# A graph-network step on one core: raw groups normalised by VectorE, and one group more brought by VectorE

## The chip, the core and the metric

The kernel runs on one core of a Trainium2 chip. The core has five engines that run their own instruction queues in order: TensorE (PE; its weight loads are PEld), VectorE (DVE), ScalarE (ACT), GpSimd (POOL) and SyncE (SP). The metric is the time of one execution in device microseconds (us). Before the change it was measured three times; the median counts. One further execution was profiled.

## The reference

12500 nodes have 128 features each; 400000 edges, sorted by their destination, have 32 features each. Each node is normalised and cut at zero, a message is made for every edge from its source, its destination and its own features, the messages of a destination are summed, and a GRU makes the new node.

```python
h = jnp.maximum(_layernorm(x, axis=-1), 0.0)
def _L0_gnn_ref(x, ei, ea, w1, b1, w2, b2, w_ih, b_ih, w_hh, b_hh):   # called with x = h
    s, d = (ei[0], ei[1])
    h = jnp.concatenate([x[s], x[d], ea], axis=-1)
    m = jax.nn.relu(h @ w1 + b1) @ w2 + b2
    agg = jax.ops.segment_sum(m, d, num_segments=x.shape[0])
    gi = agg @ w_ih + b_ih
    gh = x @ w_hh + b_hh
    i_r, i_z, i_n = jnp.split(gi, 3, axis=-1)
    h_r, h_z, h_n = jnp.split(gh, 3, axis=-1)
    r = jax.nn.sigmoid(i_r + h_r)
    z = jax.nn.sigmoid(i_z + h_z)
    n = jnp.tanh(i_n + r * h_n)
    return (1.0 - z) * n + z * x
out = x + _L0_gnn_ref(h, edge_index, edge_attr_32, ...)
```

## The kernel before

**Tiles, groups, units.** The edges are cut into 3125 tiles of 128 (T). Eight tiles are a group (PAIR); the first group has five. There are 391 groups (NP), and each is worked in two units, so a group k has the units u = 2k and 2k + 1, 782 in all (NU). The main loop runs over u. A stage of the work on a group is put a fixed number of units ahead of u: the order of every engine's queue is written out by hand (manual_schedule), and each engine works through it in order.

**A first pass over the nodes** (to about 90 us) loads x, normalises it, keeps the normalised features turned in SBUF (hT_all, 128 features x 12500 nodes), and stores A = h times the first 128 rows of w1 in DRAM.

**How a group gets the part of its messages that depends on the source.** There are four ways.
- Most groups are gathered: GpSimd issues one indirect DMA per tile (L170), which brings 128 rows of A, 512 bytes each, into a buffer G. There are eleven such buffers (GBUFS), and a gather waits until the group that had its buffer eleven places before in the ring has been used. VectorE then adds the rows to the product in PSUM and cuts at zero (L748, which writes RB).
- The first nine groups (RAW) are gathered from x itself, since A is not there yet. These are the raw groups. They need the layer norm again: raw_stats takes mean and variance of each tile on VectorE (L227, L229) and the root on ScalarE (L234), raw_fin makes scale and shift by six small VectorE instructions (L240 to L247), raw_h applies them with the cut at zero on ScalarE (relu_norm, L292, 128 columns at a time), raw_turn turns the tiles on TensorE into a PSUM bank (misc, L699) and copies that to SBUF on VectorE (gt, L701), and pre multiplies them by w1a (L727). Their cut at zero into RB is done by ScalarE (L760).
- 30 groups are brought by ScalarE, which copies single columns of hT_all, 1024 to a group (L1062, one_by_one), and 31 by VectorE, which takes two columns with one instruction (L1021, Pairs.pairs, 512 to a group) and sorts their bytes with a copy for each 128 columns (L1032). The index of each column is loaded into registers first, 32 to a load for VectorE. TensorE multiplies them by w1a, and VectorE cuts at zero (L743).
- Five groups are brought by SyncE, one DMA per row.

SPREAD says how many groups each of the three engines brings, START from which unit on it brings the first. Which groups these are follows from both: they lie evenly over the run. A group brought by VectorE must be ready at unit 2k - 6, and pairs_due spreads its 512 pairs evenly over the units since the one before. The others are GpSimd's: 325 before.

**Stages.** stages(u) puts into the queues, in this order: raw_stats(u + 7), raw_fin(u + 6) and raw_h(u + 6), raw_turn(u + 4), the products pre(u + 3), pairs before a long pass (before_long), the one-hot tiles of two groups ahead (L615, L666), the add or cut for u + 2, and pairs and a load behind it (behind_long). The main loop calls ScalarE's copies (run_jobs) in four parts around it, then the segment sums on TensorE (seg, L774), and take (L783), and every 14 groups a node step (node, 28 and a last one): sigmoid and tanh on ScalarE (L861, L873, L875), products on TensorE, and some eight passes on VectorE (L865 to L892). The loop starts at unit -7, so that the raw groups' first stages are worked ahead.

Of the kernel before, what the change touches and what calls it, by code (L numbers as in the profile page):

```python
# [9 lines left out]
F32 = mybir.dt.float32  # L10
# [7 lines left out]
ALU = mybir.AluOpType  # L18
# [5 lines left out]
GRP = 4  # L24
PAIR = 2 * GRP
# [19 lines left out]
RAW = 9  # L45
# [8 lines left out]
STEP = {"act": 4, "sp": 4}  # L54
QUEUE = 10
ROW = 4 * D
SPREAD = {"dve": 31, "act": 30, "sp": 5}
START = {"dve": 8, "act": -6, "sp": 8}
NR = 12672

H_AT = 16512
# [3 lines left out]
def tile_gnn(ctx: ExitStack, tc: tile.TileContext, x, src, srcT, dstT, dstP, eaT, eaP, w1, b1, w2T, b2,  # L65
             wih, bih, whh, bhh, out):
    nc = tc.nc
# [5 lines left out]
    p2 = ctx.enter_context(tc.tile_pool(name="p2", bufs=2))  # L73
# [4 lines left out]
    ps1 = ctx.enter_context(tc.tile_pool(name="ps1", bufs=1, space=bass.MemoryType.PSUM))  # L78
# [7 lines left out]
    def unit_tiles(u):  # L86
        k, h = divmod(u, 2)
        t0, t1 = tiles(k)
        return [(t0 + a * GRP + j, j, a) for j in (2 * h, 2 * h + 1) for a in range(2)
                if t0 + a * GRP + j < t1]  # L90

    mode, order = {}, {m: [] for m in SPREAD}
    for m, n in SPREAD.items():
        lo, hi = START[m] // 2 + 2, NP - {"dve": 5, "act": 3, "sp": 12}[m]
        for i in range(n):
# [32 lines left out]
    ident = const.tile([128, 128], F32, name="ident")  # L128
# [94 lines left out]
    def bn(pool, xs, P, n):  # L223
        b = pool.tile([128, 8, 6], F32, name="bn")
        mv = pool.tile([128, 8, 2], F32, name="mv")
        for j in range(n):
            nc.vector.bn_stats(b[:P, j, :], xs(j))  # L227
        for j in range(n):
            nc.vector.bn_aggr(mv[:P, j, :], b[:P, j, :])  # L229
        return mv  # L230

    def bn_sqrt(pool, mv, P, n):
        s = pool.tile([128, 8], F32, name="s")
        nc.scalar.activation(s[:P, :n], mv[:P, :n, 1], AF.Sqrt, bias=eps[:P, :])  # L234
        return mv, s

    def bn_fin(pool, st, mvs, P, n):
        mv, s = mvs
        y = pool.tile([128, 8], F32, name="y")
        nc.vector.reciprocal(y[:P, :n], s[:P, :n])  # L240
        v = pool.tile([128, 8], F32, name="v")
        nc.vector.tensor_scalar(v[:P, :n], mv[:P, :n, 1], 1e-5, -0.5, op0=ALU.add, op1=ALU.mult)
        nc.vector.tensor_tensor(v[:P, :n], v[:P, :n], y[:P, :n], op=ALU.mult)
        nc.vector.tensor_tensor(v[:P, :n], v[:P, :n], y[:P, :n], op=ALU.mult)
        nc.vector.scalar_tensor_tensor(st[:P, :n, 0], v[:P, :n], 1.5, y[:P, :n],
                                       op0=ALU.add, op1=ALU.mult)
        nc.vector.scalar_tensor_tensor(st[:P, :n, 1], mv[:P, :n, 0], -1.0, st[:P, :n, 0],  # L247
                                       op0=ALU.mult, op1=ALU.mult)
# [42 lines left out]
    def relu_norm(o, xi, st):  # L291
        nc.scalar.activation(o, xi, AF.Relu, bias=st[:, 1:2], scale=st[:, 0:1])  # L292
# [90 lines left out]
    with tc.tile_pool(name="pp", bufs=3) as pp:  # L383
# [22 lines left out]
        mvs, asb = {}, {}  # L406
# [186 lines left out]
    Ls, OH, RT, HE, SEG = ({} for _ in range(5))  # L593
# [14 lines left out]
    def onehot_T(k):  # L608
        if k >= NP:
            return  # L610
        c = slice((k % QP) * 512, (k % QP + 1) * 512)
        o, i = Ls[k // QP][:2 * V, c], Ls[k // QP].bitcast(I32)[:2 * V, c]
        n = k - BLOCKS[-1][0]
        if n < 0:
            nc.vector.tensor_scalar(o, i, node_of[:, k:k + 1], None, op0=ALU.is_equal)  # L615
        else:
            nc.vector.tensor_scalar(o, i, node_of[:, k:k + 1], 0.0, op0=ALU.is_equal, op1=ALU.add,
                                    accum_out=dlast[:2 * V, n:n + 1])
# [50 lines left out]
    def unit(u):  # L669
        k, h = divmod(u, 2)  # L670
        return G[k][:, 2 * h:2 * h + 2, :, :].rearrange("p j a f -> p (j a) f")


    def slots(u):
        return [(j % 2) * 2 + a for _, j, a in unit_tiles(u)]

    def raw_h(u):
        if u < 2 * RAW:
            for i, s in enumerate(slots(u)):
                relu_norm(unit(u)[:, s, :], unit(u)[:, s, :], HE[u][:, i, :])  # L680

    def raw_stats(u):
        if u < 2 * RAW:
            l = slots(u)
            HE[u] = bn_sqrt(p2, bn(p2, lambda j: unit(u)[:, l[j], :], 128, len(l)), 128, len(l))

    def raw_fin(u):
        if u < 2 * RAW:
            n = len(slots(u))
            st = p2.tile([128, GRP, 2], F32, name="st_raw", bufs=4)  # L690
            bn_fin(p2, st[:, :n, :], HE[u], 128, n)
            HE[u] = st

    def raw_turn(u):
        if u < 2 * RAW:
            l = slots(u)
            pt = ps1.tile([128, 512], F32, name="misc")
            for i, s in enumerate(l):
                nc.tensor.transpose(pt[:, i * 128:(i + 1) * 128], unit(u)[:, s, :], ident)  # L699
            hT = p3.tile([128, 512], F32, name="gt", bufs=3)  # L700
            nc.vector.tensor_copy(hT[:, :len(l) * 128], pt[:, :len(l) * 128])  # L701
            HE[u] = hT

    PP = {}
# [1 line left out]
    def pre(u):  # L706
        if u >= NU:
            return
        k, h = divmod(u, 2)
        if h == 0:  # L710
            PP[k] = ps2.tile([128, PAIR, D], F32, name="pre")
        p = PP[k][:, GRP * h:GRP * h + GRP, :]
        for i in range(2):
            c0 = (k % QP) * 512 + (2 * h + i) * 128
            raw = u in HE or k in hand
            nc.tensor.matmul(p[:, 2 * i:2 * i + 2, :], Ls[k // QP][:, c0:c0 + 128], RW[k % 4],  # L716
                             start=True, stop=not raw)
            if raw:
                l = unit_tiles(u)
                for n, (t, j, a) in enumerate(l):  # L720
                    if j % 2 == i:
                        if k in hand:
                            c = (a * GRP + j) * 128
                            cols = hand[k][:, c:c + 128]
                        else:
                            cols = HE[u][:, n * 128:(n + 1) * 128]
                        nc.tensor.matmul(p[:, 2 * i + a, :], cols, w1a, start=False,  # L727
                                         stop=n + 1 == len(l) or l[n + 1][1] != j)
# [28 lines left out]
    def relu(u):  # L757
        if u in RT:
            o, p = RT.pop(u)
            nc.scalar.activation(o, p, AF.Relu)  # L760
# [308 lines left out]
    def pairs_due():  # L1069
        start, n = START["dve"], 0  # L1070
        for k in order["dve"]:
            end = 2 * k - 6
            for u in range(start, end):
                due[u] = n + -(-(PAIR * 64 * (u + 1 - start)) // (end - start))
            n += PAIR * 64
            start = end
# [3 lines left out]
    def behind(u):  # L1080
        return due.get(u, cols.end if u >= START["dve"] else 0) - cols.done

# [4 lines left out]
    def before_long(u, ops):  # L1087
        if u == START["dve"]:
            cols.load()
        some(u, cols.end, QUEUE - ops)  # L1090
        if cols.turn and u % 2 == 0:
            some(u, cols.end, QUEUE - ops - 1)
            cols.part()

    def behind_long(u, least):
        if behind(u) >= least:
            cols.pairs(cols.left())
            cols.load()
# [9 lines left out]
    for m in ("act", "sp"):  # L1108
        start = START[m]
        for k in order[m]:  # L1110
# [39 lines left out]

    def stages(u):
        if u + 7 >= 0:
            raw_stats(u + 7)
        if u + 6 >= 0:
            raw_fin(u + 6)
            raw_h(u + 6)
        if u + 4 >= 0:
            raw_turn(u + 4)
        if u + 3 >= 0:
            pre(u + 3)  # L1160
        before_long(u, 2 if u % 4 == 2 else 1)
        if u % 2 == 0:
            onehot_T(u // 2 + 3)
            onehot(u // 2 + 3)
        if u + 2 >= 0:
            add(u + 2)
            relu(u + 2)
        behind_long(u, 1)

    nc.vector.tensor_scalar(at[:ROWS, :], at[:ROWS, :], place_of[:, 0:1], place_of[:, 1:2],  # L1170
                            op0=ALU.mult, op1=ALU.add)
    for u in range(-7, 0):
        run_jobs(u, 0)
        stages(u)
        for phase in range(1, PH):
            run_jobs(u, phase)
# [16 lines left out]
    for u in range(NU):  # L1193
        k, h = divmod(u, 2)
        gathers(u)
        if h == 0:
# [14 lines left out]
            if k == NP - 20:  # L1211
                check_windows()
        run_jobs(u, 0)
        stages(u)
        run_jobs(u, 1)
        some(u, 4, QUEUE - 1)
# [188 lines left out]
```

## Time and profile before

| | us |
|---|---|
| three runs | 3355.47, 3372.85, 3372.74 |
| their median | 3372.74 |
| the profiled execution, its own time | 3356.5 |
| its span, first to last instruction | 3354.7 |
| busy: TensorE, VectorE, ScalarE, GpSimd | 2383.9, 2429.4, 3232.5, 2509.1 |
| granted TensorE clock, share of full | 0.812 |

A row of a group reads: line, engine, operation, tile written <- tiles read, count | busy time in us, mean ns of one | idle time of the engine right before such instructions, and what ended it. A row of a wait reads: engine, tile and line that waited <- engine, tile and line that ended the wait: us in total, how often, the longest. A row of the timeline reads: start, length in us, instruction, and in brackets the idle time ahead of it. "issue" means that the engine waited for nothing that the profile shows; loads into registers are not counted as busy and appear there. A row of windows gives busy time and count of the engines in a stretch, then the granted clock, the busy share of the DMA engines and GB/s.

### The profile page before, as it was taken

How to read it: one execution, taken by the hardware profiler on the slowest of the kernel's cores; microseconds unless marked ns; L12 is line 12 of the kernel's file. 1: busy time of each engine (PE TensorE's matmuls, PEld its weight loads, DVE VectorE, ACT ScalarE, POOL GpSimd, SP SyncE). 2: the span in 40 equal slices, each digit the busy share in tenths (PEclk: the TensorE clock that was granted, in tenths of full speed). 3: DMA queues.
4: the chain of work that ended last, by engine and by line, in shares of the span. 5: the costliest groups of instructions: out<-in, count | busy, mean ns of one | idle time of the engine just before them, and what ended most of it. 6: DMA issues, size and time to landing. Idle time of an engine off the chain costs nothing. (4 is left out here: it accounts for less than half of the span.)

```text
span 3354.7 us, 98027 instructions
## 1 busy us (share of the span) xinstructions
PE 2383.9 (71%) x13209; PEld 1538.6 (46%) x13209; DVE 2429.4 (72%) x18411; ACT 3232.5 (96%) x31050; POOL 2509.1 (75%) x2606
## 2 busy tenths in 40 slices
PE   7567777766776777677677676776776676767767
PEld 6444444444444454444444444444444444434444
DVE  8467777777767777777777777767777777777775
ACT  6899999999999999999999999999999999999996
POOL 7657777777777777777777777777777777777776
PEclk9777887878877888778888878877887888888888
DMA  6323444444444443434444344444444434444332
GB/s 212 100 69 84 104 98 102 93 103 99 99 94 100 96 99 94 105 90 98 101 97 100 94 101 99 96 93 101 97 98 100 102 96 95 99 99 100 92 97 72
DMA packets 195246, 332.94 MB, mean 99 GB/s; under 512 B 68682, under 2 KB 117385, under 8 KB 194587
## 3 DMA queue, kind: packets, MB, share of 16 engines
q0 software_dynamic: 83104, 170.36, 23.3%
q1 hardware_dynamic: 111339, 156.21, 17.1%
q14 instruction: 549, 4.50, 0.4%
q8 instruction: 110, 1.80, 0.2%
q10 hardware_dynamic: 144, 0.07, 0.0%
HBM read 306.13 MB, written 20.24 MB: 97 GB/s over the span
## 5 line engine op out<-in xcount | busy, mean ns | idle before, releaser
L1062 ACT COPY HE_act<-hT_all 128x4 uint8 x30720 | 3094.2, 189 | 56.7 <-issue 29.6
L170 POOL DMA_INDIRECT G<-A,src_i x2528 | 2442.0, 966 | 806.0 <-issue 747.7
L1021 DVE SCALAR_TENSOR_TENSOR both<-hT_all 128x4 uint16 x15872 | 1353.8, 153 | 693.6 <-issue 653.6
L716 PE MATMUL pre<-RW,L 128*128 128x256 f32 x3128 | 1101.7, 476 | 9.5 <-DMA RW<-B 9.5
L774 PE MATMUL seg<-RB,OH 128*32 128x129 f32 x6250 | 599.7, 322 | 627.5 <-DVE RB L748 477.6
L716 PEld LDWEIGHTS pre<-RW,L 128*128 128x128 f32 x3128 | 646.3, 231 | 284.3 <-issue 213.1
L774 PEld LDWEIGHTS seg<-RB,OH 128*32 128x32 f32 x6250 | 330.9, 124 | 920.0 <-DVE RB L748 550.9
L748 DVE CUSTOM_DVE_ANT_0 RB<-pre,G 128x1024 f32<-128x1024 f32 (+1 forms) x317 | 383.2, 1209 | 32.0 <-PE pre L716 19.0
L615 DVE TENSOR_SCALAR L<-L,node_of 64x512 f32<-64x512 int32 x382 | 186.7, 489 | 12.0 <-DMA L<-in_dstP 12.0
L666 DVE TENSOR_TENSOR OH<-dloc,seg 128x512 f32<-128x512 f16 (+1 forms) x198 | 131.1, 662 | 0.0
L851 PE MATMUL nd<-DEG,brow 34*128 34x512 f32 (+2 forms) x112 | 72.0, 726 | 82.8 <-ACT gt L861 81.2
L806 PE MATMUL misc<-spot_h,dcol 128*128 128x40 f16 x382 | 47.4, 192 | 88.3 <-DVE dcol L831 86.3
L801 PE MATMUL nd<-spot,sums 128*128 128x40 f32 x782 | 98.7, 290 | 14.2 <-DVE sums L783 12.3
L1032 DVE COPY HE_dve<-both 128x512 uint8<-128x512 uint8 x248 | 107.5, 434 | 0.0
L801 PEld LDWEIGHTS nd<-spot,sums 128*128 128x128 f32 x782 | 93.9, 198 | 22.0 <-DVE sums L783 13.0
L727 PEld LDWEIGHTS pre<-w1a,HE_dve 128*128 128x128 f32 x496 | 87.1, 220 | 9.8
L727 PEld LDWEIGHTS pre<-w1a,HE_act 128*128 128x128 f32 x480 | 84.4, 219 | 14.2 <-ACT HE_act L1062 4.7
L727 PE MATMUL pre<-w1a,HE_act 128*128 128x128 f32 x480 | 84.3, 303 | 4.1 <-ACT HE_act L1062 4.1
L727 PE MATMUL pre<-w1a,HE_dve 128*128 128x128 f32 x496 | 86.1, 302 | 0.0
L806 PEld LDWEIGHTS <-dcol 128*128 128x128 f16 x382 | 38.8, 105 | 101.9 <-DVE dcol L831 93.8
L170 POOL DMA_INDIRECT G<-in_x,src_i x69 | 65.6, 951 | 22.2 <-issue 20.7
L743 DVE TENSOR_SCALAR RB<-pre 128x1024 f32<-128x1024 f32 x61 | 74.0, 1213 | 4.7 <-PE pre L727 4.6
(180 smaller groups left out, 1389.0 us busy)
## 6 DMA issues: line engine op xcount, KB each, us to landing
G_sp<-A SPq DMA_DIRECT2D x5120, 0.5 KB
L<-in_dstP SPq DMA_DIRECT2D x195, 256.0 KB
L<-in_eaP SPq DMA_DIRECT2D x195, 256.0 KB
G<-A,src_i POOLq DMA_INDIRECT x2528, 2.5
RW<-B SPq DMA_DIRECT2D x782, 16.0 KB
xb<-in_x SPq DMA_DIRECT2D x26, 256.0 KB
out<-xb SPq DMA_DIRECT2D x26, 256.0 KB
xs<-in_x SPq DMA_DIRECT2D x11, 512.0 KB
```

The costliest lines, as they stand in the source:

```text
L170: fetched = nc.gpsimd.indirect_dma_start(out=G[k][:, j, a, :], out_offset=None, in_=table, in_offset=bass.IndirectOffsetOnAxis(ap=src_i[c] ...
L615: nc.vector.tensor_scalar(o, i, node_of[:, k:k + 1], None, op0=ALU.is_equal)
L666: nc.vector.tensor_tensor(p, dloc[:, e0:e1, None].to_broadcast(shape), row[:, None, :].to_broadcast(shape), op=ALU.is_equal)
L716: nc.tensor.matmul(p[:, 2 * i:2 * i + 2, :], Ls[k // QP][:, c0:c0 + 128], RW[k % 4], start=True, stop=not raw)
L727: nc.tensor.matmul(p[:, 2 * i + a, :], cols, w1a, start=False, stop=n + 1 == len(l) or l[n + 1][1] != j)
L748: made = nc.vector._custom_dve(TENSOR_ADD_SAT, out=o, in0=p, in1=G[k].rearrange("p j a f -> p (j a) f")[:, c, :], s0=float("inf"), s1=0.0)
L774: nc.tensor.matmul(p[r0:r0 + V, :D + 1], OH[k][:, a * GRP + j, :], RB[k % 2][:, 2 * j + a, :D + 1], start=False, stop=all(b != a for _, _, ...
L801: nc.tensor.matmul(p[:, bass.ds(offs[i], V + SHIFT)], sums[:, slot(b, i), :D], spot[:, i % 2, :], start=False, stop=i == len(offs) - 1)
L806: nc.tensor.matmul(p[:, bass.ds(offs[i], V + SHIFT)], t[:, c:c + 128], spot_h[:, a, :], start=False, stop=i == len(offs) - 1)
L1021: nc.vector.scalar_tensor_tensor(self.both[:, e % PIECE // 2, :], column(second), 256.0, column(first), op0=ALU.mult, op1=ALU.add)
L1032: nc.vector.tensor_copy(hand[k].bitcast(U8)[:, p0 * 4:(p0 + PIECE) * 4].rearrange("p (n c b) -> p n c b", c=2, b=4), both.bitcast(U8).rear ...
L1062: nc.scalar.copy(he[:, e * 4:e * 4 + 4], column(v))
```

## The change

VectorE, not ScalarE, applies scale and shift to the raw groups, with one tensor_scalar for each tile; the cut at zero moves to the copy behind the transposes, which becomes a tensor_scalar with a maximum. Statistics, roots and scales are made for two units at a time, at even units. The statistics are put eight units ahead instead of seven, the roots stand in stages of their own a unit behind, and the first statistics are put ahead of the loop. The copy of turned tiles goes from raw_turn to raw_copy at the end of a stage, ahead of behind_long. VectorE brings 32 groups and GpSimd gathers 324; VectorE's first pairs are made from unit 10 on, not 8. Its groups are now 18, 30, 42, 54, ... 374, 386; the first is 18 and the last 386 in both kernels. Where a number is already taken, some of ScalarE's 30 groups shift by one; SyncE's stay.

```diff
-SPREAD = {"dve": 31, "act": 30, "sp": 5}
-START = {"dve": 8, "act": -6, "sp": 8}
+SPREAD = {"dve": 32, "act": 30, "sp": 5}
+START = {"dve": 10, "act": -6, "sp": 8}
...
+    def raw_stats(u):
+        if u % 2 == 0 and u < 2 * RAW:
+            l = [(v, s) for v in (u, u + 1) for s in slots(v)]
+            HE[u] = bn(p2, lambda i: unit(l[i][0])[:, l[i][1], :], 128, len(l)), len(l)
+
+    def raw_sqrt(u):
+        if u % 2 == 0 and u < 2 * RAW:
+            mv, n = HE[u]
+            HE[u] = bn_sqrt(p2, mv, 128, n), n
+
+    def raw_fin(u):
+        if u % 2 == 0 and u < 2 * RAW:
+            mvs, n = HE[u]
+            st = p2.tile([128, PAIR, 2], F32, name="st_raw")
+            bn_fin(p2, st[:, :n, :], mvs, 128, n)
+            HE[u], HE[u + 1] = st[:, :len(slots(u)), :], st[:, len(slots(u)):, :]
+
     def raw_h(u):
         if u < 2 * RAW:
             for i, s in enumerate(slots(u)):
-                relu_norm(unit(u)[:, s, :], unit(u)[:, s, :], HE[u][:, i, :])
-
-    def raw_stats(u):
-        if u < 2 * RAW:
-            l = slots(u)
-            HE[u] = bn_sqrt(p2, bn(p2, lambda j: unit(u)[:, l[j], :], 128, len(l)), 128, len(l))
-
-    def raw_fin(u):
-        if u < 2 * RAW:
-            n = len(slots(u))
-            st = p2.tile([128, GRP, 2], F32, name="st_raw", bufs=4)
-            bn_fin(p2, st[:, :n, :], HE[u], 128, n)
-            HE[u] = st
+                nc.vector.tensor_scalar(unit(u)[:, s, :], unit(u)[:, s, :], HE[u][:, i, 0:1], HE[u][:, i, 1:2],
+                                        op0=ALU.mult, op1=ALU.add)
 
     def raw_turn(u):
         if u < 2 * RAW:
             l = slots(u)
-            pt = ps1.tile([128, 512], F32, name="misc")
+            HE[u] = ps1.tile([128, 512], F32, name="misc")
             for i, s in enumerate(l):
-                nc.tensor.transpose(pt[:, i * 128:(i + 1) * 128], unit(u)[:, s, :], ident)
+                nc.tensor.transpose(HE[u][:, i * 128:(i + 1) * 128], unit(u)[:, s, :], ident)
+
+    def raw_copy(u):
+        if u < 2 * RAW:
+            n = len(slots(u)) * 128
             hT = p3.tile([128, 512], F32, name="gt", bufs=3)
-            nc.vector.tensor_copy(hT[:, :len(l) * 128], pt[:, :len(l) * 128])
+            nc.vector.tensor_scalar(hT[:, :n], HE[u][:, :n], 0.0, None, op0=ALU.max)
             HE[u] = hT
...
     def stages(u):
         if u + 7 >= 0:
-            raw_stats(u + 7)
+            raw_sqrt(u + 7)
+        raw_stats(u + 8)
         if u + 6 >= 0:
             raw_fin(u + 6)
             raw_h(u + 6)
...
             relu(u + 2)
+        if u + 4 >= 0:
+            raw_copy(u + 4)
         behind_long(u, 1)
...
+    raw_stats(0)
     for u in range(-7, 0):
         run_jobs(u, 0)
         stages(u)
```

## The prediction

> **What bounds the kernel now.** I read the busy shares first, then the idle time of each engine and what ended it, and then single stretches of the timeline.
>
> ```profile
> span 3354.7 us, 98027 instructions
> PE 2383.9 (71%) x13209; PEld 1538.6 (46%) x13209; DVE 2429.4 (72%) x18411; ACT 3232.5 (96%) x31050; POOL 2509.1 (75%) x2606
> ...
> L1062 ACT COPY HE_act<-hT_all 128x4 uint8 x30720 | 3094.2, 189 | 56.7 <-issue 29.6
> L170 POOL DMA_INDIRECT G<-A,src_i x2528 | 2442.0, 966 | 806.0 <-issue 747.7
> L1021 DVE SCALAR_TENSOR_TENSOR both<-hT_all 128x4 uint16 x15872 | 1353.8, 153 | 693.6 <-issue 653.6
> ```
>
> ScalarE is full: its copies leave 56.7 us of idle time in the whole run. GpSimd shows 75%, but its gathers are issued back to back. VectorE shows 72%, but 653.6 us of its idle time stands in front of the pair instructions of L1021 and is ended by "issue": it waits there for no other engine, but for its own loads of 32 registers. So three engines are near their limits, and the question is which of them has slack, and where.
>
> ```profile
> core 0: us, PE busy (x) PEld busy (x) DVE busy (x) ACT busy (x) POOL busy (x), PEclk, DMA share, GB/s
> 130.00:200.00 70.00, 47.55 (x272) 37.79 (x268) 38.33 (x237) 69.77 (x534) 43.14 (x46) 0.78 0.30 72
> 290.00:3300.00 3010.00, 2153.18 (x11936) 1359.80 (x11937) 2212.25 (x17103) 2952.11 (x29011) 2288.12 (x2368) 0.81 0.41 98
> ```
>
> In the raw stage (130 to 200 us) ScalarE alone is busy, 69.77 of 70 us; VectorE has 38.33, TensorE 47.55. From 290 us on ScalarE is busy 2952.11 of 3010 us.
>
> ```profile
> POOL G L170 <- issue: 768.5, 2519, 0.6
> POOL G L170 <- DVE RB L748: 21.5, 18, 12.1
> POOL G L170 <- PE misc L699: 16.1, 5, 4.0
> ...
> POOL G L170 <- ACT G L292: 1.7, 1, 1.7
> ...
> 231.38 0.95 POOL L170 DMA_INDIRECT G<-A,src_i  x1 [12.06 <-DVE RB L748]
> ...
> 3337.08 0.94 POOL L170 DMA_INDIRECT G<-A,src_i  x1 [0.30 <-issue]
> ...
> 3345.04 0.44 ACT L950 ACTIVATE gt<-pre 128x320 f32<-128x320 f32 x1 [19.85 <-PE pre L931]
> ```
>
> GpSimd waits for buffers of G for 21.5 + 16.1 + 1.7 = 39.3 us in 24 gaps; 0.3 us of each is its usual gap, so 32 us are true stalls, nearly all before 270 us. Its last gather is issued at 3337.08, 17 us before the end, so GpSimd also ends late. ScalarE's last copies are over some 20 us before 3345.
>
> ```profile
> DVE gt L865 <- ACT gt L861: 40.7, 11, 6.2
> DVE RB L748 <- PE pre L716: 19.0, 10, 4.3
> DVE RB L748 <- DMA G<-A,src_i: 12.7, 4, 4.4
> L743 DVE TENSOR_SCALAR RB<-pre 128x1024 f32<-128x1024 f32 x61 | 74.0, 1213 | 4.7 <-PE pre L727 4.6
> ```
>
> This is all that VectorE waits for others in the long stage that could vanish: 40.7 + 19.0 + 12.7 + 4.6 = 77 us. The first two come from a late ScalarE (a sigmoid queued behind its copies, and TensorE held up by it), the third from GpSimd. VectorE's slack is thus 77 us in 3100, 2.5%.
>
> **Part 1, normalising moves to VectorE, roots are halved.**
>
> ```profile
> L1062 ACT COPY HE_act<-hT_all 128x4 uint8 x340 | 34.0, 190 | 0.2
> L292 ACT ACTIVATE G<-G,st_raw 128x128 f32<-128x128 f32 x32 | 13.1, 478 | 0.0
> L760 ACT ACTIVATE RB<-pre 128x1024 f32<-128x1024 f32 x5 | 5.0, 1000 | 0.0
> L234 ACT ACTIVATE s<-mv,eps 128x4 f32<-128x4 f32 x8 | 2.3, 293 | 0.0
> L240 DVE RECIPROCAL y<-s 128x4 f32<-128x4 f32 x6 | 1.1, 178 | 19.3 <-ACT s L234 19.3
> ...
> ACT s L234 <- DVE mv L229: 4.6, 1, 4.6
> ```
>
> The first four rows are ScalarE from 142 to 193 us, eight units: 51 us, 6.4 each. The rows sum to 54.4, as records overlap a little; 51 / 54.4 = 0.94 puts them on the clock. L292 goes (13.1 x 0.94 / 8 = 1.5 a unit), half of the roots go (0.14), so a raw unit costs ScalarE 4.7. Up to unit 10 that is 61 tiles at 0.385 (23.5 us), some five roots (1.4) and the 4.6 us in which it waited for the first statistics, which are now made a unit earlier: 29 us. With all 69 tiles and nine roots it is 34. TensorE is no obstacle: 47.55 / 70 x 6.4 = 4.3 a unit. VectorE spends 38.33 / 70 x 6.4 = 3.5 a unit there and waits 19.3 us in six units for roots. Gone is half of the six small instructions (0.5 a unit); new are four normalisations of 128 columns. No row has them; between the 0.147 us of an aggregation and the 0.489 of the 64x512 pass I take 0.2, close to the statistics of the same tile:
>
> ```profile
> L227 DVE BATCH_NORM_STATS2 bn<-G 128x6 f32<-128x128 f32 x69 | 14.9, 273 | 0.0
> L229 DVE BATCH_NORM_AGGREGATE mv<-bn 128x2 f32<-128x6 f32 x167 | 14.1, 147 | 0.0
> L615 DVE TENSOR_SCALAR L<-L,node_of 64x512 f32<-64x512 int32 x382 | 186.7, 489 | 12.0 <-DMA L<-in_dstP 12.0
> ```
>
> That makes 3.5 - 0.5 + 0.8 = 3.8 a unit, under ScalarE's 4.7: hidden. At 0.489 it is 5.0, and VectorE would set the unit at a loss of 0.3 x 16 = 5 us; without any cover the 69 instructions cost 14 us (10 to 34). So part 1 gives -29, between -34 and -22 (29 less 5, and 2 for the price of a normalisation). The roots asked a unit ahead wait for nothing new. Behind a root in ScalarE's queue stand the copies of its unit, but the statistics are one unit old by then.
>
> **Part 2, turned tiles copied at a stage's end.** The copy from PSUM (18 of them) gets a maximum instead of a plain copy; the same kind of pass at twice the size takes 1.213 us, so about 0.65, as now. It stands behind the one-hot tiles and the pairs, so VectorE no longer stops for the transposes; the next unit's transposes need its PSUM bank, and wait for it at most that unit's rest. 0, between -5 (one such wait of 4.7 in the raw stage) and +3.
>
> **Part 3, pairs start at unit 10, not 8.**
>
> ```profile
> 182.03 0.60 DVE L1021 SCALAR_TENSOR_TENSOR both<-hT_all 128x4 uint16 x7 [1.79 <-issue]
> ```
>
> VectorE made its first pairs at 182 us, in unit 8. Now its first group has 20 units instead of 22. Up to unit 30 that is 46 pairs more than it had there, 3 loads' worth, against statistics that are over: +4 us by the prices of part 4. In this stretch VectorE is the full engine, so these stand on the path.
>
> **Part 4, one group from GpSimd to VectorE.** GpSimd loses 8 gathers of 0.966 + 0.304 us, 10.2 us. VectorE gains 512 pairs. By the rows: 1353.8 / 31 = 43.7 us of instructions, 653.6 / 31 = 21.1 us of stall, and the eight copies of L1032, 107.5 / 31 = 3.5; 68 us. The add is replaced by a pass of the same length (1.213 against 1.209), nothing. What one more load costs is bounded by these:
>
> ```profile
> L748 DVE CUSTOM_DVE_ANT_0 RB<-pre,G 128x1024 f32<-128x1024 f32 (+1 forms) x317 | 383.2, 1209 | 32.0 <-PE pre L716 19.0
> L1032 DVE COPY HE_dve<-both 128x512 uint8<-128x512 uint8 x248 | 107.5, 434 | 0.0
> ...
> 1506.64 0.60 DVE L1021 SCALAR_TENSOR_TENSOR both<-hT_all 128x4 uint16 x7 [1.33 <-issue]
> ...
> 1513.44 0.60 DVE L1021 SCALAR_TENSOR_TENSOR both<-hT_all 128x4 uint16 x7 [0.27 <-issue]
> ```
>
> A load behind a one-hot pass leaves 0.27 us open, one behind nothing but pairs and a short copy 1.33. The places behind long passes are shared by more loads now, so 32 loads cost between the average (21) and 32 x 1.33 = 43: the group costs 68 to 90, plus an eighth (9 to 11) for the 64 pairs made ahead of unit 10 until now. I take 78, of which 4 are part 3, since the same code that places 31 groups' loads behind long passes places these; 74 remain beyond unit 30, at most 97.
>
> What hides them are the 77 us of waits above: VectorE comes later, so ScalarE's sigmoids and GpSimd's rows are there. Net 0 if all goes, +20 if one load in two is fully exposed and none of the rest is hidden better. But ScalarE has no slack either (2952.11 of 3010 us). Two full engines that meet at 28 node steps don't lag in the same stretches: the waits now come up to 6.2 us each; I estimate one or two such swings that are not absorbed, +8, between 0 and +30.
>
> **A rule that speaks against it.** Gathers take longer while VectorE makes pairs:
>
> ```profile
> L170 POOL DMA_INDIRECT G<-A,src_i x39 | 36.8, 945 | 23.6 <-PE misc L699 12.9 <-issue 10.7
> ...
> L170 POOL DMA_INDIRECT G<-A,src_i x158 | 152.5, 965 | 48.2 <-issue 46.7 <-DVE RB L748 0.3 <-DVE both L1021 0.3
> ```
>
> They take 945 ns from 140 to 200 us and 965 from 700 to 900. The Trainium skill, "SBUF — State Buffer", section "Who interferes with whom", says that VectorE in a two-port mode (a copy or a tensor_scalar) locks GpSimd out of the port they share for the whole instruction, descriptors of its DMAs included. By that rule the 69 normalisations could delay GpSimd by 69 x 0.2 = 14 us; the 20 ns agree with the direction, not with whole instructions. GpSimd's own limit would then be -28 instead of the -42 of the next part, still below the sum, so it would touch only the rival that runs to all limits.
>
> **The sum.** The profiled execution took 3356.5 us, span 3354.7. Limits alone: GpSimd -10 - 32 = -42, ScalarE -34, VectorE -29 + 78 - 77 = -28. With the steps in order: -29 + 0 + 4 + 74 - 74 (of the 77) + 8 = **-17**, or 3339.5 us. The three runs are 3355.47, 3372.85 and 3372.74; the profiled one is like the lowest, 16 below the median, and the page doesn't show what sets the others apart. I give 3345, between 3339.5 and its counterpart 17 higher, nearer the first.
>
> **Rivals.**
> A, every engine runs to its limit: the waits of VectorE vanish and nothing swings. ScalarE's -34 decides, 3322 us (3328 by the rule of the skill). For it: GpSimd never waits after 270 us. Against: two saturated queues that meet.
> B, the start gain is eaten: VectorE's extra 74 to 97 us find only 60 of cover, since VectorE and ScalarE wait for each other in turn. -25 + 14 to 37 + 8 = -3 to +20: 3357 to 3389 with the two kinds of run, no change that can be told. For it: the waits sit at few places (11 and 10). That TensorE, 4.3 us of work in a raw unit, stretches these to 5.5 gives the same: half of the 29 gone.
> C, slower: VectorE becomes the bound for the whole run. The mechanism: each of the 36 added loads (32 and the four of part 3) lies bare at 1.33 us, 101 us in all, the 40.7 us of waits on sigmoids stay, as ScalarE's steps are still queued behind its copies, and only 36 go. -22 + 101 - 36 = +43: 3399 us. It decides when VectorE's extra exceeds its vanished waits by more than 29 + 17 = 46. For it: VectorE's true slack is only 2.5%, and a group is 2.2 to 2.9%. Against: a ScalarE that is 25 us ahead isn't late at the sigmoids.
>
> **Chances.** Forecast (3325 to 3356) 0.40; A 0.08; B 0.33; C 0.19. A measurement of this kernel tells 0.5% (17 us) from no change, so faster means below 3356 and slower above 3389. The upper end of the forecast reads as no change in a run of the slower kind (0.02): faster 0.46, same 0.35, slower 0.19. The range reaches from A's limit, 3320, to C's 3399.
>
> **What would show it.** Right: raw units of about 4.7 us on ScalarE; the first add of L748 near 205 instead of 230 us; GpSimd's stalls on L699 and L748 near nothing; L865's wait on L861 well under 40.7 us; stall ahead of L1021 some 25 to 45 us more. Wrong: a raw unit above 5.5 us, waits of ScalarE that weren't there (for TensorE or HE_act), a wait on L861 as before, or gathers above 980 ns.

## The result, and the profile after

| | kernel before | changed kernel |
|---|---|---|
| median of 12 runs | 3371.41 us (3355.47 to 3377.27) | 3367.68 us (3362.58 to 3372.33) |
| profiled execution | 3356.5 us | 3362.58 us |
| first add of a gathered unit | 229.9 us | 212.8 us |
| last gather issued | 3337.08 us | 3311.70 us |

The ratio of the mean times is 0.9996, with a 95% interval of 0.9983 to 1.0008 (the two medians alone give 0.9989): no change that can be told, where 3345 us had been forecast. The time lies where rival B put it (3357 to 3389). The start did become shorter, by 17 us up to the first add, and by the end nearly all of it was gone. TensorE's granted clock, 0.812 in the profile before and 0.801 in this one, doesn't explain that: over the 12 runs of the changed kernel it lies between 0.801 and 0.815, and the run with 0.801 is the fastest.

The first lines of the changed kernel's page and its costliest groups. A line of the diff's functions stands 10 lines lower than before (L1021 is now L1031, L748 is L758, L861 and L865 are L871 and L875), the normalisation is L697:

```profile
span 3360.8 us, 98514 instructions
PE 2394.7 (71%) x13225; PEld 1550.7 (46%) x13225; DVE 2485.5 (74%) x18946; ACT 3205.5 (95%) x30972; POOL 2500.7 (74%) x2598
...
L1072 ACT COPY HE_act<-hT_all 128x4 uint8 x30720 | 3093.6, 189 | 57.0 <-issue 28.6
L170 POOL DMA_INDIRECT G<-A,src_i x2520 | 2433.7, 966 | 789.3 <-issue 741.6
L1031 DVE SCALAR_TENSOR_TENSOR both<-hT_all 128x4 uint16 x16384 | 1397.0, 153 | 726.0 <-issue 684.3
...
L1042 DVE COPY HE_dve<-both 128x512 uint8<-128x512 uint8 x256 | 111.6, 436 | 0.2 <-issue 0.2
```

Against the same rows before, the group that VectorE took over cost it 1397.0 - 1353.8 = 43.2 us of pair instructions, 684.3 - 653.6 = 30.7 of stall at its loads and 111.6 - 107.5 = 4.1 of copies: 78.0 us. Now the waits of the engines (who for whom, us in total, number, longest), and behind them one of the kernel before:

```profile
ACT gt L883 <- DVE gt L879: 22.8, 8, 7.1
...
POOL G L170 <- DVE RB L758: 20.8, 19, 8.5
...
DVE gt L711 <- PE misc L705: 8.3, 3, 7.9
ACT RB L770 <- PE pre L737: 8.0, 1, 8.0
DVE RB L753 <- PE pre L737: 6.3, 2, 4.3
...
ACT gt L871 <- PE nd L865: 6.0, 4, 3.3
DVE RB L758 <- PE pre L726: 5.6, 4, 3.1
...
DVE gt L875 <- ACT gt L871: 3.3, 2, 2.2
...
POOL G L170 <- PE misc L705: 2.8, 1, 2.8
```

```profile
ACT gt L873 <- DVE gt L869: 0.7, 2, 0.5
```

VectorE's four waits of 77 us have become 3.3 + 5.6 + 6.3 = 15.2, and the one for GpSimd's rows (12.7) is not there any more: 62 us of cover were used. In exchange ScalarE, which waited 0.7 us in all for VectorE's pass in the node steps (L869, now L879), waits 22.8 us for it, and 8.0 us for TensorE at the start. Its busy time fell by 3232.5 - 3205.5 = 27.0 us, the span grew by 6.1, so its idle time grew by 33: it has given back all that it was relieved of. VectorE's account is 56.1 us more busy and 30.7 more stall at L1031, against 80.7 less of all other idle time: together the 6.1 us. Of the 80.7, 62 are the four waits, and 21.4 are the raw stage's waits for roots (L240 for L234), which fell from 33.3 to 11.9. That VectorE is the engine that binds is a reading so far; the first experiment tests it. GpSimd is out of it: its last gather went from 18 to 49 us before the end.

And the start, on the timelines (start, duration, in brackets the idle time before it). TensorE, VectorE and ScalarE of the changed kernel in the first fence, SyncE's queue of the changed kernel in the second, TensorE of the kernel before in the third:

```profile
119.09 1.19 PE L726 MATMUL pre<-RW,L 128*128 128x256 f32 x2 [9.44 <-DMA RW<-B]
...
123.31 0.69 DVE L711 TENSOR_SCALAR gt<-misc 128x512 f32<-128x512 f32 x1 [7.86 <-PE misc L705]
...
124.88 1.02 ACT L770 ACTIVATE RB<-pre 128x1024 f32<-128x1024 f32 x1 [8.00 <-PE pre L737]
...
135.95 8.49 ACT L1072 COPY HE_act<-hT_all 128x4 uint8 x84
...
183.50 8.82 ACT L1072 COPY HE_act<-hT_all 128x4 uint8 x88
```

```profile
94.48 4.84 SPq L107 DMA_DIRECT2D L<-in_eaP  x1
101.17 28.84 SPq L107 DMA_DIRECT2D RW<-B  x12
```

```profile
117.15 1.19 PE L716 MATMUL pre<-RW,L 128*128 128x256 f32 x2 [9.45 <-DMA RW<-B]
```

The first matrix product of the raw units needs window rows (RW) of B, which SyncE asks for at 101.17 us, behind the six L loads of three units, one of which holds its queue for 4.84 us. The product that waits for them starts at 119.09. The kernel before waited for the same rows, until 117.15, but ScalarE was then still normalising and copying and noticed nothing. The changed ScalarE is earlier, runs into this wait and stands for 8.0 us; VectorE stands with it for 7.9. After that the raw stage is as fast as forecast: from 135.95 to 183.50 us lie ten units (ScalarE's two rows are the copies behind the cut of a whole group, two units each), 4.76 us each.

### The profile page after: what moved, and what is told of

Read it like the earlier page. It is cut to its first block, busy times and chain, and to the rows that moved or that the text cites. A ratio compares the mean times of both kernels' runs of the same rounds, so it can differ in the third digit from the quotient of the medians.

```text
span 3360.8 us, 98514 instructions
## 1 busy us (share of the span) xinstructions
PE 2394.7 (71%) x13225; PEld 1550.7 (46%) x13225; DVE 2485.5 (74%) x18946; ACT 3205.5 (95%) x30972; POOL 2500.7 (74%) x2598
## 3 DMA queue, kind: packets, MB, share of 16 engines
q1 hardware_dynamic: 111341, 156.21, 17.1%
## 5 line engine op out<-in xcount | busy, mean ns | idle before, releaser
L1031 DVE SCALAR_TENSOR_TENSOR both<-hT_all 128x4 uint16 x16384 | 1397.0, 153 | 726.0 <-issue 684.3
L726 PE MATMUL pre<-RW,L 128*128 128x256 f32 x3128 | 1115.4, 481 | 9.4 <-DMA RW<-B 9.4
L726 PEld LDWEIGHTS pre<-RW,L 128*128 128x128 f32 x3128 | 655.2, 234 | 286.3 <-issue 222.6
L758 DVE CUSTOM_DVE_ANT_0 RB<-pre,G 128x1024 f32<-128x1024 f32 (+1 forms) x316 | 382.0, 1209 | 5.8 <-PE pre L726 5.6
L615 DVE TENSOR_SCALAR L<-L,node_of 64x512 f32<-64x512 int32 x382 | 186.5, 488 | 5.6 <-DMA L<-in_dstP 5.6
L1042 DVE COPY HE_dve<-both 128x512 uint8<-128x512 uint8 x256 | 111.6, 436 | 0.2 <-issue 0.2
L816 PEld LDWEIGHTS <-dcol 128*128 128x128 f16 x382 | 39.1, 105 | 116.8 <-DVE dcol L841 106.5
L861 PE MATMUL nd<-DEG,brow 34*128 34x512 f32 (+2 forms) x112 | 66.3, 674 | 9.0 <-ACT gt L871 8.9
```

Of the source, the lines that this page charges most:

```text
L758: made = nc.vector._custom_dve(TENSOR_ADD_SAT, out=o, in0=p, in1=G[k].rearrange("p j a f -> p (j a) f")[:, c, :], s0=float("inf"), s1=0.0)
L816: nc.tensor.matmul(p[:, bass.ds(offs[i], V + SHIFT)], t[:, c:c + 128], spot_h[:, a, :], start=False, stop=i == len(offs) - 1)
L1031: nc.vector.scalar_tensor_tensor(self.both[:, e % PIECE // 2, :], column(second), 256.0, column(first), op0=ALU.mult, op1=ALU.add)
L1042: nc.vector.tensor_copy(hand[k].bitcast(U8)[:, p0 * 4:(p0 + PIECE) * 4].rearrange("p (n c b) -> p n c b", c=2, b=4), both.bitcast(U8).rear ...
```

## The experiments

Two theories stood against each other. **V**: after the start VectorE is the bound, the 32nd group costs what it was sized at and its cover is smaller than 77 us, and a wait of TensorE for RW takes part of the start's gain. **Rivals**: VectorE's normalising has made the raw stage or GpSimd slower, or the place of the copy or of the roots, or ScalarE, sets the end. The times are medians; the kernel before took 3370.25 us beside the first four kernels and 3371.02 beside the next four. The rows come from one profiled execution of each kernel.

**One group back to GpSimd (raw31).** The changed kernel with 31 groups on VectorE:

```
-SPREAD = {"dve": 32, "act": 30, "sp": 5}
+SPREAD = {"dve": 31, "act": 30, "sp": 5}
```

> The changed kernel with 31 groups on VectorE instead of 32 (START stays 10), so GpSimd gathers 325 again. Theory V: the raw part of the change gained about 17 us (the first add of a gathered group came 17 us earlier), and the 32nd group cost VectorE 78 us (43 of instructions, 31 of stall, 4 of byte sorting), of which waits hid only some 62; without it VectorE has slack again and ScalarE's line, 17 us earlier than before, carries to the end: 3350 to 3358 us, and VectorE waits again for L871 some 30 us or more. Rival S: two saturated queues lose the early gain on the way, whatever VectorE brings: 3364 to 3372, with the first gathered add 17 us early and no gain left by 2000 us.

Measured: 3343.15 us (3340.39 to 3346.31), ratio to the kernel before 0.9919 (0.9906 to 0.9933), 24.5 us less than the changed kernel and below V's 3350 to 3358. Its waits, and in the second fence its groups of pairs and of their copies:

```profile
DVE gt L875 <- ACT gt L871: 24.2, 12, 5.4
DVE RB L758 <- DMA G<-A,src_i: 23.0, 8, 5.0
...
DVE RB L758 <- PE pre L726: 14.9, 12, 4.5
...
ACT gt L883 <- DVE gt L879: 7.7, 3, 4.5
...
DVE RB L753 <- PE pre L737: 6.2, 4, 4.3
```

```profile
L1031 DVE SCALAR_TENSOR_TENSOR both<-hT_all 128x4 uint16 x15872 | 1357.9, 156 | 689.8 <-issue 646.4
...
L1042 DVE COPY HE_dve<-both 128x512 uint8<-128x512 uint8 x248 | 108.3, 437 | 0.0
```

The four waits are back, 68.3 us. So with the other three parts in place the 32nd group found 68.3 - 15.2 = 53 us of cover, against a cost of 39.1 + 37.9 + 3.3 = 80 us by the differences of the same three rows as above: 27 us on the path, where the spans of the profiles differ by 22.2 and the medians by 24.5. So VectorE is the bound of the changed kernel: with one group less it is faster, though GpSimd has eight gathers more. ScalarE waits for VectorE a third as long as there.

**The group alone (b32).** The kernel before with 32 groups on VectorE, still starting at unit 8:

```
-SPREAD = {"dve": 31, "act": 30, "sp": 5}
+SPREAD = {"dve": 32, "act": 30, "sp": 5}
```

> The kernel of before with 32 groups on VectorE (START 8, raw stage as before). Theory V: no start gain; 70 to 78 us more for VectorE, about 60 hidden by its waits: 10 to 18 us slower than before, 3381 to 3389. Rival S (the group is hidden like other VectorE work, and the early gain was lost anyway): within 5 us of before. Rival G: GpSimd sets the end of the kernel of before, so 8 gathers fewer make it 10 us faster.

Measured: 3383.6 us (3375.93 to 3389.25), ratio 1.0042 (1.0028 to 1.0056), 13 us slower, as V has it. Its wait of ScalarE for VectorE, VectorE's own waits, and its groups of pairs and of their copies, one fence each:

```profile
ACT gt L873 <- DVE gt L869: 14.8, 8, 3.6
```

```profile
DVE RB L743 <- PE pre L727: 8.0, 4, 4.3
...
DVE RB L748 <- PE pre L716: 3.4, 3, 2.7
...
DVE gt L865 <- ACT gt L861: 3.0, 2, 2.0
```

```profile
L1021 DVE SCALAR_TENSOR_TENSOR both<-hT_all 128x4 uint16 x16384 | 1400.7, 156 | 728.7 <-issue 685.6
...
L1032 DVE COPY HE_dve<-both 128x512 uint8<-128x512 uint8 x256 | 111.7, 436 | 0.0
```

VectorE's wait for gathered rows is gone, the one for sigmoids is down to 3.0, and ScalarE waits for VectorE. The four waits are 14.4 us, so here too 77 - 14.4 = 62.6 were used as cover; the cost by the three rows is 46.9 + 32.0 + 4.2 = 83.1, which leaves 20.5 on the path, where the profiled executions differ by 19.4 and the medians by 13.4. So the cover was too small for the group alone, without the rest of the change.

By the medians the group costs 13 us alone and 24.5 in company; the rest alone gives 27 (that the pairs start at unit 8 here decides nothing, by a run further down). As a sum of parts taken alone the change would give -14, and it gives -4. By the rows that is because the two draw on the same slack, 62.6 us of it alone and 53 in company. The profiled executions say the same with a smaller number, 19.4 alone and 22.2 in company, so how much the parts take from each other is known only roughly, 3 to 11 us.

**The window rows asked for first (rwfirst).** In the changed kernel, RW's loads go ahead of the L loads of the second and third unit:

```
-    for q in range(3):
-        fetch(q)
+    fetch(0)
...
+    for q in range(1, 3):
+        fetch(q)
```

> The changed kernel, with the first four groups' window rows (RW) asked for ahead of the second and third load of L instead of behind them. In the changed kernel TensorE waits 9.4 us for RW until 119.1 us, and ScalarE and VectorE wait for TensorE, 8.0 and 7.9 us. Theory V: TensorE starts 6 to 10 us earlier, these waits shrink to under 2 us, the first gathered add comes 6 to 8 us earlier, and as VectorE is full from then on all of it stays: 3358 to 3363 us. Rival S: lost on the way, 3365 to 3370.

Measured: 3358.94 us (3354.93 to 3360.83), ratio 0.9965 (0.9951 to 0.9979), 8.7 us less than the changed kernel. Its first product on the timeline, its adds of gathered units (shortest, median and longest in ns, then first and last start), and ScalarE's wait for VectorE, one fence each:

```profile
108.95 1.06 PE L726 MATMUL pre<-RW,L 128*128 128x256 f32 x2
```

```profile
L758 DVE CUSTOM_DVE_ANT_0 RB<-pre,G x316: 683/1219/1225, 204.6 to 3334.1; 128x1024 f32<-128x1024 f32 x157, 128x512 f32<-128x512 f32 x1
```

```profile
ACT gt L883 <- DVE gt L879: 24.7, 7, 6.3
```

The product starts ten microseconds earlier, with no wait in front of it; ScalarE's 8.0 us are gone, and the first gathered add comes at 204.6 us, where the prediction looked for it. What the start lost to RW was 212.8 - 204.6 = 8.2 us. The later wait for VectorE stays as it was.

**Both (raw31rw).** 31 groups and RW first (the edits of the two kernels above together):

> Both edits: 31 groups on VectorE, and the first window rows ahead of the second load of L. Theory V: 6 to 8 us below raw31, 3343 to 3352 us, unless GpSimd (one group more, its stalls near 200 us) holds the end, then 3348 to 3355 with its last gather within 20 us of the end. Rival S: as raw31 without it, 3364 to 3372.

Measured: 3331.77 us (3329.9 to 3341.59), ratio 0.9893 (0.9875 to 0.991), below the 3343 to 3352 that V expected. Its adds of gathered units:

```profile
L758 DVE CUSTOM_DVE_ANT_0 RB<-pre,G x317: 691/1219/1226, 200.8 to 3313.4; 128x1024 f32<-128x1024 f32 x158, 128x512 f32<-128x512 f32 x1
```

The first is at 200.8 us, 29.1 earlier than before the change and 3.8 earlier than with 32 groups. With 31 groups VectorE's first one is 19, not 18, so fewer pairs are made ahead of that add: 167 up to 200.7 us, where rwfirst has 182 up to 204.5. At 78 us for 512 pairs these 15 make an estimated 2.3 us; the rest of the 3.8 is not accounted for. At the end the two edits add up (8.7 + 24.5 = 33.2, measured 35.9).

**Normalising back on ScalarE (normact)**, in that kernel:

```
-                nc.vector.tensor_scalar(unit(u)[:, s, :], unit(u)[:, s, :], HE[u][:, i, 0:1], HE[u][:, i, 1:2],
-                                        op0=ALU.mult, op1=ALU.add)
+                relu_norm(unit(u)[:, s, :], unit(u)[:, s, :], HE[u][:, i, :])
```

> As raw31rw (31 groups, window rows first), but ScalarE applies scale and shift to the raw groups again (cut at zero included); the paired roots, the later copy and the earlier statistics stay. Theory V: the start gain comes from ScalarE's 69 passes, 0.385 us each: 26 us of ScalarE come back, the first gathered add is 20 to 26 us later than in raw31rw, and most of it stays: 3345 to 3356 us. Rival P: the gain came from the halved roots, the statistics a unit earlier and the moved copy: then 3328 to 3338.

Measured: 3363.43 us (3353.0 to 3365.81), 31.7 more than with the passes on VectorE and above the 3345 to 3356 that V expected. ScalarE's normalisations and the first gathered add:

```profile
L292 ACT ACTIVATE G<-G,st_raw 128x128 f32<-128x128 f32 x69 | 28.4, 480 | 2.4 <-DVE st_raw L247 2.4
```

```profile
L757 DVE CUSTOM_DVE_ANT_0 RB<-pre,G x317: 691/1214/1225, 222.8 to 3334.8; 128x1024 f32<-128x1024 f32 x158, 128x512 f32<-128x512 f32 x1
```

The 69 passes are 28.4 us of ScalarE, the first add is 22.0 us later than in raw31rw, and the end 31.7 by the medians, 23.1 between the profiled executions (3353.0 and 3329.9), from which the rows are. This kernel has the paired roots, the earlier statistics and RW first, and is 7.6 us below the kernel before: those three together, with the pairs from unit 10 on, are worth no more than that where ScalarE normalises.

**The copy inside the turn (copyturn).** Again in the kernel with both edits, the copy from PSUM is made right behind the transposes, as before the change:

```
+            raw_copy(u)
...
-        if u + 4 >= 0:
-            raw_copy(u + 4)
```

> As raw31rw, but the copy out of PSUM stands right behind the transposes again, inside raw_turn. Theory V: it costs nothing on the way that sets the end, 3327 to 3336 us. Rival P: VectorE stops for the transposes in each raw unit (one such wait of 4.7 us in the kernel of before), 5 to 10 us slower, 3337 to 3345.

Measured: 3330.74 us (3323.21 to 3336.68), ratio 0.9885 (0.987 to 0.99), against 3331.77. The place of the copy is worth nothing that can be told.

**Pairs from unit 8 again (s8)**, in the changed kernel:

```
-START = {"dve": 10, "act": -6, "sp": 8}
+START = {"dve": 8, "act": -6, "sp": 8}
```

> The changed kernel (32 groups) with VectorE's first pairs from unit 8 on, not 10. Theory V: VectorE is the bound from about unit 17 on, so the 46 or so pairs that move from the full stretch into units 8 and 9, where VectorE still waits for ScalarE's roots, come off the end: 4 to 6 us faster than the changed kernel, 3361 to 3365. Rival: VectorE has no slack in units 8 and 9 either, so nothing changes, 3366 to 3369.

Measured: 3366.87 us (3360.34 to 3371.28), like the changed kernel. V missed here: the pairs made two units earlier pushed the first gathered add back to 216.6 us and gave the same at the end. So VectorE has no empty place in units 8 and 9: what the early pairs cost at the first add, 3.8 us, is also what they save behind it, and no more.

**One group fewer (raw30rw)**, 30 on VectorE, RW first:

```
-SPREAD = {"dve": 31, "act": 30, "sp": 5}
+SPREAD = {"dve": 30, "act": 30, "sp": 5}
```

> As raw31rw with 30 groups on VectorE, so GpSimd gathers 326. Theory V, continued: with 31 GpSimd holds the end again (VectorE waits 15.9 us for rows, last gather 17 us before the end), so 8 gathers more cost their 10 us: 3338 to 3344 us, VectorE's waits for rows well above 16 us. Rival: VectorE is still part of the bound, and 78 us less on it make it faster: 3318 to 3328.

Measured: 3336.74 us (3334.73 to 3337.91), 5 more than with 31 and just below the 3338 that V expected at least. Its waits of VectorE:

```profile
DVE gt L875 <- ACT gt L871: 66.8, 18, 9.4
DVE RB L758 <- DMA G<-A,src_i: 52.8, 24, 5.0
```

VectorE, one group lighter, now waits 120 us for ScalarE and GpSimd in these two places, where raw31rw has 26.8 + 15.9, and GpSimd has eight gathers more. With 30 groups VectorE waits for the others, with 32 one of them waits for VectorE; 31 lies between.

**Inconclusive: RW first in the kernel before (brw, brw2, brw3), and the changed kernel once more (copyturn32).** If ScalarE's normalising covers the wait for RW there, the same edit should give the kernel before nothing. It was run three times, and the changed kernel, unaltered, once beside it, where the kernel before took 5885 to 5944 us.

> The kernel of before, with the first four groups' window rows asked for ahead of the second and third load of L, as in rwfirst. There too TensorE waits 9.5 us for them, until 117.2 us, but ScalarE, the full engine of its raw stage, waits for TensorE nowhere near. Theory V: the wait is covered by ScalarE's normalising, so the first gathered add and the time stay within 3 us of before, 3367 to 3373. Rival W: the wait delays the start of both kernels alike, then 8 to 11 us faster, 3359 to 3363, and the missing part of the start gain in the changed kernel has another cause.

> As brw, again: in brw's runs the kernel of before itself took 5944 us, with ScalarE's copies issued one by one for long stretches, so its raw stage was not the one in question. Where the kernel of before takes about 3370: theory V, the wait for the window rows is covered by ScalarE's normalising, within 3 us of before. Rival W: 8 to 11 us faster, and the missing part of the start gain has another cause.

> As brw and brw2, in the hope of the kernel of before at about 3370 us beside it. Theory V: TensorE's 9.5 us wait for the window rows is covered by ScalarE's normalising, within 3 us of before. Rival W: 8 to 11 us faster, and the missing part of the start gain in the changed kernel has another cause.

> The changed kernel once more, beside brw2 on the same chip: 3365 to 3370 us, if the chip is as in the first runs.

Measured, as ratios to the kernel before: 0.9989 (0.998 to 0.9999), 1.0004 (0.9993 to 1.0016) and 0.9999 (0.9987 to 1.0012) for the edit, 0.9921 (0.9897 to 0.9946) for the changed kernel. The edit gives nothing in these runs, but they say little of the case: one of them in the profile (ScalarE's copies as a group, then two neighbouring ones on the timeline):

```profile
L1062 ACT COPY HE_act<-hT_all 128x4 uint8 x30720 | 3366.9, 189 | 2277.8 <-issue 2246.5
```

```profile
926.15 0.19 ACT L1062 COPY HE_act<-hT_all 128x4 uint8 x1 [1.21 <-issue]
927.55 0.19 ACT L1062 COPY HE_act<-hT_all 128x4 uint8 x1 [1.20 <-issue]
```

ScalarE's copies were as short as ever, but for long stretches came one in 1.40 us, which puts a bound on the kernel that is none elsewhere. Whether the kernel before would gain from RW first under the conditions of the other runs stays open. Two things suggest that the gain would be small: in the trace of before ScalarE doesn't wait for that product, and normact, which has RW first beside other parts of the change, gained 7.6 us in all.

## Why the prediction was wrong

**The step that failed first in time** is "TensorE is no obstacle: 47.55 / 70 x 6.4 = 4.3 a unit". As an average from 130 us on it was right, and the raw unit came out at 4.76 us where 4.7 was predicted. But the start of the stage isn't in that window. TensorE's wait for RW, 9.45 us, stood in the trace of before at 107 to 117 us and cost nothing there that shows, since ScalarE was late. Part 1 counted 29 us from ScalarE's work alone, and the first gathered add came 17.1 earlier. Of the 12 that are missing, 8.2 are TensorE's wait (rwfirst), and 3.8 more came with 31 groups. That the two together make 29.1 is luck to a tenth: the later start of the pairs is in it, which is worth 3.8 us at this add by itself (s8). So the start was 8 too large.

**The second term that failed, and the larger,** is the cover, "Net 0 if all goes". Of the cover of 77 us only 62 were used up; 15 stayed. Part 4's cost was right, 78 taken and 78.0 measured, though the 78 was a choice near the low end of 77 to 101 and the pairs of runs above give 80 and 83, so the exact hit is luck. That leaves 16 us exposed where the sum had 4. The condition was written down ("ScalarE has no slack either") but priced at 8. What the runs show in its place: the cover was too small for the group alone, which cost 13 us by the medians and 19.4 between the profiles (b32). And it shrinks once ScalarE is relieved: 68 us of waits are then left, of which the 32nd group uses 53; what remains exposed is 27 by these rows, and the times say 22 to 24.5. Two things each laid claim to the same waits, an earlier ScalarE and a later VectorE.

**Rival B** came nearest. Its main mechanism, that VectorE's extra finds only 60 us of cover since VectorE and ScalarE wait for each other in turn, is what was measured: 62, with new waits of ScalarE. Its other reading, a TensorE that stretches the raw units to 5.5 us, did not happen: the units took 4.76, and all were delayed once.

**The sum with these terms**: -29 + 8 for the start, 78 - 62 for parts 3 and 4 and their cover, and the 8 for swings make +3, where the profiled executions differ by +6.1. Only the 8 of the start and the 78 and 62 are measured in it. The 8 for swings was not; ScalarE's 22.8 us of waiting for VectorE, up to 7.1 at a time, show that ScalarE is held up, not what that costs. The two profiled executions were each among the fastest of their kernel: 15 below the median before, 5 after. Between the profiles the change is therefore +6.1 and between the medians -3.7; ten of what the sum says lie in that choice. It also decides how the miss is shared out. By the profiles the changed kernel with 31 groups is 16 us faster than the kernel before, 9 short of the -25 of parts 1 to 3. By the medians it is 27 faster, so nothing is missing there, and the whole miss lies in the 32nd group's 24.5. That the cover failed holds either way; that the start fell short is shown at the first add, and by the 8.7 us that rwfirst won back at the end.

**What was right.** The normalisations were hidden by VectorE's slack in the raw stage: they took 0.341 us by the record (median) and 0.256 from one start to the next (0.2 taken), and VectorE was busy 38.49 of the 50 us from 135 to 185, 3.7 us a unit (3.8 predicted). The 69 passes:

```profile
L697 DVE TENSOR_SCALAR G<-G,st_raw x69: 326/341/557, 95.5 to 181.6; 128x128 f32<-128x128 f32 x69
```

Part 2 was zero, as said (copyturn). Part 3's 4 us weren't to be seen: moving the start back returned nothing (s8). The price was inconsistent besides: 46 pairs at part 4's 78 us for 512 are 7 us, and part 4 counts 64 pairs for the same place. Of the signs named, L865's wait came down to 3.3 us and the stall at L1021 grew by 30.7, as said; new waits of ScalarE, named as a sign of being wrong, were the one that decided. GpSimd's last gather came 25.4 us earlier: the 10.2 of its eight gathers and 15 of its stalls, where 32 were predicted to vanish; some 17 remained, the longest 8.5 us behind a late first add. This cost nothing, as GpSimd was never late again.

**The rule on the port.** Gathers between 140 and 180 us, while VectorE normalised, and below them those of the kernel before in the same stretch:

```profile
L170 POOL DMA_INDIRECT G<-A,src_i x33 | 31.6, 956 | 10.1 <-issue 9.1 <-DVE bn L227 0.6 <-PE pre L737 0.3
```

```profile
L170 POOL DMA_INDIRECT G<-A,src_i x28 | 26.4, 943 | 13.9 <-issue 7.9 <-PE misc L699 5.9
```

The rule of the Trainium skill, "SBUF — State Buffer", section "Who interferes with whom", would have a gather wait for whole normalisations of 0.341 us, if these ran in a two-port mode. Whether they did, no run here shows. The trace gives 13 ns more for a gather, 0.4 us over the 33, and one gather holds most of it:

```profile
146.86 1.21 POOL L170 DMA_INDIRECT G<-A,src_i  x1 [0.30 <-issue]
```

It took 0.27 us more than the one behind it, while VectorE made a one-hot pass (L615). Waits for whole normalisations are not to be seen, and GpSimd was not the bound.

**Rival C**, VectorE as the bound, came true as a mechanism and not in its price: the added group cost 30.7 + 43.2 + 4.1 = 78 instead of 101, and the waits on sigmoids went, which it let stay. **Rival A**, every engine at its limit, was excluded by ScalarE's new waits.

**A version that beats both** comes out of this: RW's loads ahead of the second unit's L loads, VectorE's normalising, 31 groups on VectorE: 3331.77 us, ratio 0.9893 (0.9875 to 0.991), and 3330.74 (0.987 to 0.99) with the copy in the turn.

## What to carry to other kernels

Slack on one engine that comes from another's lateness can be spent once: if a change relieves the late engine and loads the waiting one in the same step, take the waits that would be left after the first and set the load against those, not against the waits of the profile. Nor do all waits give way: 14 to 15 of 77 us stayed here, with the group alone and with the whole change. Before counting a saving on a full engine, read what the other engines waited for under it at the same place, from its first use on: a wait of 9.45 us that cost nothing was the next bound, and one moved load removed it. And measure a group's place with one step to either side, 30, 31 and 32 here, since the best lay where two engines meet: with RW first 3336.74, 3331.77 and 3358.94 us.

## What was unexpected of the hardware

The kernel before, 3370 us elsewhere, took 5885 to 5944 us in the last runs, on three chips that none of the other experiments ran on, with a granted clock near 0.67; in the one trace shown, single ScalarE copies come 1.40 us apart while their own duration stays at 0.19 us. The cause was not found.
